# A decoder layer on one Trainium2 core: the first weight scales spread by one-hot matmuls, two weight products moved to GpSimd

## The chip, the core and the metric

The kernel runs on one core of a Trainium2 chip. A core has five engines that run on their own and wait for each other through semaphores: TensorE (PE; its weight loads are shown apart, as PEld), VectorE (DVE), ScalarE (ACT), GpSimd (POOL) and SyncE (SP), which here only issues transfers. ScalarE issues some transfers too. The on-chip memory SBUF has 128 partitions; TensorE writes its results to PSUM, which VectorE and ScalarE read. The metric is the time of one execution on the device in microseconds (us); lower is better. The time before is 569.73 us, the median of 3 runs (569.17 to 570.04).

## What is computed

A decoder layer on 1024 tokens (16 sequences of 64) of width 256, in f32: self-attention with 16 heads of 128, cross-attention to a context of width 64, and a mixture of 16 experts with 4 chosen per token, each behind a layer norm and added to its input. The change touches the first step alone, the projections of self-attention, whose weights come as codes with one scale for each block of 32 input rows:

```python
def _layernorm(x, axis=-1, eps=1e-05):
    m = jnp.mean(x, axis=axis, keepdims=True)
    v = jnp.var(x, axis=axis, keepdims=True)
    return (x - m) / jnp.sqrt(v + eps)

def _mxfp4_matmul(x, codes, scales, block_size=BLOCK):
    w = codes * jnp.repeat(scales, block_size, axis=0)
    return x @ w

q = _mxfp4_matmul(x, wq_codes, wq_scales) + bq
k = _mxfp4_matmul(x, wk_codes, wk_scales) + bk
v = _mxfp4_matmul(x, wv_codes, wv_scales) + bv
...
x = x + _L0_attn_ref(_layernorm(x, axis=-1), ...)
x = x + _L0_xattn_ref(_layernorm(x, axis=-1), ctx_512, ...)
x = x + _L0_ffn_ref(_layernorm(x, axis=-1), ...)
```

## The kernel before, in words

**Tiles.** The tokens lie in 8 tiles of 128 partitions by 256 features, taken in two halves of four tiles. The layer norm of a half (`layernorm_t`, L159) goes through: statistics of four tiles on VectorE (L170, L171), the variance plus epsilon (`ln_var`, L174), its power of -0.5 on GpSimd (`ln_rstd`, L177), `ln_shift` = -mean times `ln_rstd` on VectorE (L181), then the normed tiles `ln_x`, two on ScalarE and two on VectorE (L199, L192), eight 128x128 transposes on TensorE (L216), and for each 128 features a high part rounded on ScalarE (L222) and a low part, the rest, on VectorE (L224). TensorE multiplies both parts by the weights, so that little of f32 is lost.

**Weights of self-attention.** The heads go in groups of two. For each group the weights of q, k, v and o are `code` times `scale`, both 128 partitions by 512 columns (`multiply`, L509; the product at L514), on VectorE for q and k, and for v of the first group; otherwise on GpSimd. `load_weights` (L495) fetches both by SyncE: codes at L501, scales at L502. In memory the scales are held for 16 rows and spread over 128 partitions by the transfer, 8 partitions to a row. The pools hold three `code` and three `scale` tiles.

**Start.** Six transfers bring x, three from SyncE and three from ScalarE. TensorE has nothing to do yet and turns the identity over (`turn_idly`, L133): 22 transposes ahead of the real ones and 14 between the first half's transposes and its first product. `first_queries` (L612) is called inside the layer norm of the second half: it loads the first group's weights and begins the product of q with the first half (`head_qk_part`, L543, whose matmuls are at L104). After that the loop over heads runs: queries and keys (L551 is their bias on ScalarE), scores (L565), softmax (L324 to L334), transposes of the probabilities (L343), values (L582, L592), projection (L605).

**Order.** A planner places each instruction in its engine's queue when the program is built; `tc.issue_after`, used through `after` (L95), tells it to place an instruction behind another one. Each engine then works through its queue in this fixed order, so an instruction that waits holds up all behind it on its engine. A change in the first microseconds can also change the planner's choices later; it does so in the layer norm ahead of cross-attention, whose rope products are `rt` on VectorE (L976) and `roped` on GpSimd (L982), read by TensorE at L997.

**Names that the change touches.** `turn_idly(22)` at L137; `load_weights`, `multiply`, `first_queries`; `at_tile` (L89), the PSUM tiles of the scores, of which two exist; `raw_tile` (L359), raw weight tiles that are first used by cross-attention; the lists `variances`, `rstds`, `norms`, `scaled` and `lows`, in which `layernorm_t` records instructions for `after`.

## Time and profile before

| | |
|---|---|
| median of 3 runs | 569.73 us |
| the profiled execution | 570.74 us, of which 569.0 us are the span of its trace |
| granted TensorE clock, mean of the span | 0.984 |
| transfers by SyncE's queue | 58.71 MB, 34.7% of the 16 engines' span |
| transfers by ScalarE's queue | 1.05 MB, 0.6% |
| TensorE in the first 5 us / 5 to 10 / 10 to 15 / 15 to 20 | busy 1.86 / 5.00 / 4.03 / 5.00 us |
| TensorE's longest waits | 6.4 us in 2 for VectorE near the end, 3.1 us for the identity at the start |

The page of a profile gives busy times by engine, the span in 40 slices, the chain of waits that ended last, and groups of instructions. The trace behind it can be asked for a stretch of time. A row of the timeline reads: start and duration in us, engine, line, operation, output<-input, shape, count; then in brackets how long the engine stood idle before it and what it waited for. Instructions of one kind that follow each other are one row, with the time from the first one's start to the last one's end. A TensorE record is longer than the distance to the next one, since they overlap; distances tell the rate.

### The profile page before, as it was taken

How to read it: one execution, taken by the hardware profiler on the slowest of the kernel's cores; microseconds unless marked ns; L12 is line 12 of the kernel's file. 1: busy time of each engine (PE TensorE's matmuls, PEld its weight loads, DVE VectorE, ACT ScalarE, POOL GpSimd, SP SyncE). 2: the span in 40 equal slices, each digit the busy share in tenths (PEclk: the TensorE clock that was granted, in tenths of full speed). 3: DMA queues.
4: the chain of work that ended last, by engine and by line, in shares of the span. 5: the costliest groups of instructions: out<-in, count | busy, mean ns of one | idle time of the engine just before them, and what ended most of it. 6: DMA issues, size and time to landing. Idle time of an engine off the chain costs nothing.

```text
span 569.0 us, 10603 instructions
## 1 busy us (share of the span) xinstructions
PE 537.4 (94%) x4013; PEld 444.5 (78%) x4013; DVE 400.9 (70%) x879; ACT 279.3 (49%) x524; POOL 230.5 (41%) x213
## 2 busy tenths in 40 slices
PE   7999999999999998999999999999999879999961
PEld 6888898988989876667687676676788779999961
DVE  5456555644555788767485686888878678999876
ACT  4677556575565533131323324143445368777551
POOL 4160500102000104434441445453445738888862
PEclk9999999999999999999999999999999989999995
DMA  8654431724300499564010000000322667776374
GB/s 213 163 170 129 129 106 44 205 95 108 97 1 1 119 289 277 140 188 127 2 52 20 8 1 1 0 30 1 105 106 80 209 217 255 244 249 239 123 272 164
DMA packets 44262, 70.83 MB, mean 124 GB/s; under 512 B 11824, under 2 KB 25232, under 8 KB 44208
## 3 DMA queue, kind: packets, MB, share of 16 engines
q1 hardware_dynamic: 39376, 58.71, 34.7%
q0 software_dynamic: 3696, 10.36, 4.7%
q10 hardware_dynamic: 1136, 1.05, 0.6%
q8 instruction: 33, 0.54, 0.4%
q14 instruction: 21, 0.17, 0.1%
HBM read 48.61 MB, written 21.86 MB: 124 GB/s over the span
## 4 chain that ended last, share of the span: by engine, by line
PE 76%; DVE 11%; DMA 4%; issue 3%; ACT 3%; POOL 1%; SPq 0%; DVEq 0%; ACTq 0%; POOLq 0%
PE mm L104 45%; PE mm L997 7%; PE av L582 5%; PE at L565 4%; PE av L104 3%; PE at L343 3%; PE at L1020 2%; PE av L1033 2%; PE mm L431 2%; DMA yd<-y,to 2%; ACT w L278 1%; DMA w<-in_W 1%; DVE hp L113 1%; DVE w L283 1%; DVE x L1326 1%
## 5 line engine op out<-in xcount | busy, mean ns | idle before, releaser
L982 POOL TENSOR_TENSOR roped<-rt,rt 128x512 f32<-128x512 f32 x48 | 62.6, 1326 | 83.3 <-DVE rt L976 80.4
L976 DVE TENSOR_TENSOR rt<-mm,rope_q 128x512 f32<-128x512 f32 x96 | 61.4, 684 | 24.3 <-PE mm L104 23.6
L104 PE MATMUL mm<-xn,w_q 128*128 128x512 f32 x288 | 73.9, 403 | 0.5 <-ACT xn L222 0.5
L104 PEld LDWEIGHTS mm<-xn,w_q 128*128 128x128 f32 x288 | 52.2, 188 | 14.1 <-issue 1.8
L104 PE MATMUL mm<-xs,w 128*128 128x384 f32 x270 | 54.2, 348 | 6.0 <-ACT xs L112 3.0
L1296 POOL DMA_INDIRECT yd<-y,to x45 | 48.7, 1082 | 19.4 <-ACT y L1291 8.0
L104 PEld LDWEIGHTS mm<-xs,w 128*128 128x128 f32 x270 | 47.0, 193 | 8.3 <-ACT xs L112 4.0
L327 ACT ACTIVATE p<-p 128x512 f32<-128x512 f32 x32 | 20.1, 629 | 62.3 <-DVE p L326 62.3
L324 DVE TENSOR_REDUCE sm_m<-at 128x8 f32<-128x512 f32 x32 | 21.8, 680 | 36.1 <-PE at L565 35.2
L997 PE MATMUL mm<-roped,w_s 128*64 128x512 f32 x192 | 46.4, 601 | 0.7 <-POOL roped L982 0.7
L514 POOL TENSOR_TENSOR wv<-code,scale 128x512 fp32r<-128x512 f32 x7 | 9.0, 1282 | 87.4 <-DMA scale<-in_scales 50.3
L605 DVE TENSOR_TENSOR x<-mm,x 128x256 f32<-128x256 f32 x64 | 26.0, 419 | 24.0 <-PE mm L104 22.8
L104 PE MATMUL mm<-wo,o 128*128 128x256 f32 x256 | 39.6, 295 | 0.0
L104 PE MATMUL mm<-xn,wq 128*128 128x512 f32 x128 | 34.6, 404 | 0.7 <-ACT xn L222 0.5
L104 PE MATMUL av<-w,hp 128*128 128x256 f32 x225 | 35.0, 289 | 0.3 <-ACT y L1291 0.3
L104 PE MATMUL mm<-wv,xn 128*128 128x256 f32 x256 | 35.2, 288 | 0.0
L104 PE MATMUL mm<-xn,wk 128*128 128x512 f32 x128 | 34.9, 405 | 0.0
L582 PE MATMUL av<-pt,v 128*128 128x128 f32 x256 | 34.5, 277 | 0.0
L104 PEld LDWEIGHTS mm<-wo,o 128*128 128x128 f32 x256 | 32.9, 190 | 1.5 <-issue 0.4
L582 PEld LDWEIGHTS av<-pt,v 128*128 128x128 f32 x256 | 32.0, 191 | 1.2
L104 PEld LDWEIGHTS mm<-wv,xn 128*128 128x128 f32 x256 | 31.8, 189 | 0.9
L514 POOL TENSOR_TENSOR wo<-code,scale 128x512 fp32r<-128x512 f32 x8 | 10.9, 1368 | 52.0 <-PE mm L104 39.6
(216 smaller groups left out, 1163.8 us busy)
## 6 DMA issues: line engine op xcount, KB each, us to landing
w<-in_W SPq DMA_DIRECT2D x15, 640.0 KB, 4.2
code<-in_codes SPq DMA_DIRECT2D x32, 256.0 KB, 4.4
scale<-in_scales SPq DMA_DIRECT2D x32, 256.0 KB, 4.9
xr<-xd SPq DMA_DIRECT2D x15, 408.0 KB, 4.9
xd<-zeros SPq DMA_DIRECT2D x8, 720.0 KB, 6.8
yd<-zeros SPq DMA_DIRECT2D x8, 512.0 KB, 6.6
got<-yd SPq DMA_DIRECT2D x16, 256.0 KB, 3.6
wq<-in_Wq SPq DMA_DIRECT2D x4, 512.0 KB, 3.7
```

Source lines behind the costliest of these rows:

```text
L104: m = nc.tensor.matmul(ps, lhsT=l, rhs=r, start=(n == 0), stop=(n == len(pairs) - 1))
L324: nc.vector.tensor_reduce(m, sc, AX.X, ALU.max)
L327: exps.append(nc.scalar.activation(p, p, AF.Exp, scale=scale).ins)
L343: last = nc.tensor.transpose(ps[:, 2 * n : 2 * n + 2, :].rearrange("p a q -> p (a q)"), pn[:, 2 * n : 2 * n + 2, :].rearrange("p a k -> p ...
L514: mults[n] = eng.tensor_tensor(w, *loaded[gr].pop(n), ALU.mult).ins
L565: nc.tensor.matmul(sc[par * 64 : par * 64 + 64, 2 * g + pp, :], lhsT=qk[0][:, b * S : (b + 1) * S], rhs=qk[1][:, b * S : (b + 1) * S], sta ...
L582: nc.tensor.matmul(av[:, k * 128 : (k + 1) * 128], lhsT=v[:, i, k0 : k0 + HD], rhs=pt[:, i].rearrange("p a q -> p (a q)"), start=True, sto ...
L605: nc.vector.tensor_tensor(x[i], ps, x[i], ALU.add)
L976: nc.vector.tensor_tensor(mt, ps3, rope_table(t, 2 * ab + k), ALU.mult)
L982: nc.gpsimd.tensor_tensor(r.rearrange("p (b s) -> p b s", s=S), one, two, op)
L997: nc.tensor.matmul(ps[h // 2][(h % 2) * 64 : (h % 2) * 64 + 64], lhsT=w_s[:, t, blk, ab, :], rhs=roped[2 * t + ab], start=first[h], stop=l ...
L1296: sent = nc.gpsimd.indirect_dma_start(out=yd[: (E - 1) * SLOTS + min(TOPK, E - 1 - e) * NT], out_offset=bass.IndirectOffsetOnAxis(ap=to[:, ...
```

## The change

For the first group, `load_first_weights` takes the place of `load_weights`. The scales of q, k and v come as the four rows that they have for each 128 input rows, with a 4 by 128 block matrix that has a one in row r for the partitions 32r to 32r+31; two small transfers on ScalarE's queue fetch them into raw tiles. TensorE multiplies the block matrix by the four rows, which gives the scale of each partition, in PSUM, in two tiles used in turn. q's product reads its scales in PSUM. Those of k and v are copied to SBUF by ScalarE, and GpSimd multiplies these two weights. The first 22 idle transposes become 10 and another 8 that stand with the loads. The order of q's, k's and v's products is asked for behind other instructions than before.

```diff
-    turn_idly(22)
+    turn_idly(10)
...
+            def load_first_weights():
+                first = raw_tile("wkq", [4, 1, 640])
+                nc.scalar.dma_start(out=first[:, 0], in_=a["scales_first"][:, :640])
+                others = raw_tile("wq", [4, 2, 512])
+                nc.scalar.dma_start(
+                    out=others,
+                    in_=a["scales_first"][:, 640:].rearrange("r (n c) -> r n c", n=2),
+                )
+                for n, rows in (("q", first[:, 0, 128:]), ("k", others[:, 0]), ("v", others[:, 1])):
+                    code = sw.tile([128, 2, 256], F32, tag="code", name="code", bufs=3)
+                    loads.append(nc.sync.dma_start(out=code, in_=a["codes"][0, :, "qkvo".index(n)]).ins)
+                    scale = at_tile([128, 2, 256])
+                    nc.tensor.matmul(
+                        scale.rearrange("p c n -> p (c n)"),
+                        lhsT=first[:, 0, :128],
+                        rhs=rows,
+                        start=True,
+                        stop=True,
+                    )
+                    if n != "q":
+                        ps = scale
+                        scale = sw.tile([128, 2, 256], F32, tag="scale", name="scale", bufs=3)
+                        nc.scalar.copy(scale, ps)
+                    loaded.setdefault(0, {})[n] = code, scale
+                turn_idly(8)
+
             def multiply(gr, names, *order):
                 for n in names:
                     w = sw.tile([128, 2, 256], F32R, tag=f"w{n}", name=f"w{n}")
-                    eng = nc.vector if n in "qk" or n == "v" and gr == 0 else nc.gpsimd
+                    eng = nc.vector if n == "q" or n == "k" and gr else nc.gpsimd
...
             def first_queries(xn_h):
                 with after(turned[-1]):
                     turn_idly(14)
-                load_weights(0, "qk")
-                multiply(0, "q", variances[1])
-                multiply(0, "k", scaled[3], lows[1])
+                multiply(0, "q", norms[3])
+                multiply(0, "k", rstds[0])
                 nc.sync.dma_start(out=bqkv, in_=a["bqkv"])
-                load_weights(0, "v")
...
+            load_first_weights()
             xn_t = layernorm_t(1, meanwhile=first_queries)
-            multiply(0, "v", lows[3])
+            multiply(0, "v", rstds[1])
...
+    blocks = np.repeat(np.eye(4, dtype=np.float32), 32, axis=1)
+    arrays["scales_first"] = np.concatenate(
+        [blocks, arrays["scales"][0, :, :3].reshape(4, 3 * 512)], axis=1
+    )
     arrays["scales"] = np.repeat(arrays["scales"], 4, axis=1)
```

## The prediction

> **What bounds the kernel now.** I read the page's table of engines and the clock row first, then the chain of waits, then TensorE's waits by stage, then the timeline of the first 17 us (start, duration, engine, line, operation, count, and in brackets the idle time before it and who ended it).

> ```profile
> span 569.0 us, 10603 instructions
> PE 537.4 (94%) x4013; PEld 444.5 (78%) x4013; DVE 400.9 (70%) x879; ACT 279.3 (49%) x524; POOL 230.5 (41%) x213
> ```

> TensorE is the bound: busy for 537.4 of 569.0 us, and 76% of the chain. Its waits between 15 and 210 us add up to nothing; all its waiting lies before 14.04 us, around 211 to 228, and in the expert stage after 393. So whatever puts off the moment at which TensorE's unbroken stream begins puts off the end by as much, and only waits in those three places can be won. This is the beginning:

> ```profile
> 3.14 4.88 PE L135 MATMUL av<-ident 128*128 128x128 f32 x22 [3.14 <-POOL ident masks.py:199]
> 7.85 1.04 PE L216 MATMUL mm<-ident,ln_x 128*128 128x128 f32 x8
> 8.72 1.69 PE L135 MATMUL av<-ident 128*128 128x128 f32 x14
> 9.55 0.17 DVE L174 TENSOR_SCALAR ln_var<-ln_mv 128x4 f32<-128x4 f32 x1
> 9.74 0.69 DVE L514 TENSOR_TENSOR wq<-code,scale 128x512 fp32r<-128x512 f32 x1
> 9.79 1.50 POOL L177 TENSOR_TENSOR ln_rstd<-ln_var,half_power 128x4 f32<-128x4 f32 x1 [3.00 <-DVE ln_var L174]
> 10.35 1.28 DVE L224 TENSOR_TENSOR xn<-mm,xn 128x512 fp32r<-128x512 f32 x2
> 11.55 0.15 DVE L181 SCALAR_TENSOR_TENSOR ln_shift<-ln_mv,ln_rstd 128x4 f32<-128x4 f32 x1
> 11.79 1.09 ACT L199 ACTIVATE ln_x<-x,ln_shift,ln_rstd 128x256 f32<-128x256 f32 x2 [2.00 <-issue]
> 12.79 0.67 ACT L551 ACTIVATE qT<-mm,bqkv 128x512 f32<-128x512 f32 x1
> 13.40 1.08 ACT L222 CAST xn<-mm 128x512 fp32r<-128x512 f32 x2
> 14.04 0.50 PE L104 MATMUL mm<-xn,wq 128*128 128x512 f32 x1 [0.46 <-ACT xn L222]
> ```

> Read it backwards from 14.04: the stream begins when ScalarE has written the first high part of the second half (first of the two at 13.40). That waits on ScalarE for qT and the two ln_x, these for ln_shift on VectorE (11.55), this for the reciprocal deviation on GpSimd (9.79 to 11.29) and for VectorE's own queue. The weight transfers are not what ends last: VectorE was at ln_var until 9.72, and q's scales landed at 9.63 (2.63 plus 7.0 to landing); k's scales landed at 12.07, when VectorE was at ln_x until 12.47; v's at 14.55, and v's product stood at 15.23 behind other work. **The three scale loads are hidden, by 0.1, 0.3 and 0.7 us.**

> **The change, part by part.** The order of the built program gives what follows what on each engine.

> *Transfers.* Three loads of 256 KB leave SyncE's queue, two small ones (10 and 16 KB) join ScalarE's. That saves VectorE no wait (above). They cost ScalarE two issues of 0.4 us near 2.1 and 3.4, before its table load; it needs its first input at 7.03: nothing. Codes of k and v, bqkv and the next group land about 1 to 4 us earlier; nobody waits there: nothing. The small loads stand in the queue behind the last x load, issued at 1.66 and landed by 8.3 at the latest, where VectorE uses it; so I put them at 7.0 to 8.0.

> *VectorE.* It loses k's and v's products (0.68 each). The first lay before an idle 0.95, the second behind all that TensorE waits for: nothing. q's product now reads PSUM (0.68, as the 96 products at L976 that also read PSUM) and stands before ln_var instead of behind it, so ln_var ends at about 10.35 instead of 9.72. In exchange the reciprocal deviation, which took 1.50 beside that product and 1.04 without it, takes 1.04: it ends at 11.4 instead of 11.3. Nearly nothing.

> *Three one-hot products on TensorE,* f32, 4 rows by 512 columns, in its queue between the idle transposes and the real ones. The nearest row is the f32 product of 192 columns:

> ```profile
> L431 PE MATMUL mm<-wkq,wq x64: 323/326/431, 176.0 to 289.0; 128*128 128x192 f32 x64
> ```

> The 64 records stand for 32 products, each two records 0.16 apart, so 0.32 us for 192 columns and 0.86 for 512. [...]I take the row, since it is the same type; only its 128 rows differ. Of the idle transposes four go (18 instead of 22 ahead of the real ones, ending at 7.0 at the unwarmed spacing of 0.213). Then q's product, 7.5 to 8.5; four transposes (0.109 each); k's, 0.86; four more, to 10.2; 14 idle ones, 1.5; v's, to 12.6. [...]

> *Two more copies on ScalarE.* k's scales are copied ahead of the first half's high parts (10.0 to 10.6, moving these from 8.71 to 10.5), v's ahead of qT. By 11.5 the second high part is there, as the queues need; but the copy ahead of qT stands in the chain above: one 128x512 copy, +0.48 (the spacing of the two at L222).

> *GpSimd multiplies k's and v's weights,* 1.28 each (L514). k's stands right behind the second reciprocal deviation, and ln_shift on VectorE waits for that same instruction. ln_shift has two operands in SBUF. Where it ran beside a GpSimd product before, in the last layer norm:

> ```profile
> 372.91 0.93 DVE L181 SCALAR_TENSOR_TENSOR ln_shift<-ln_mv,ln_rstd 128x4 f32<-128x4 f32 x1
> ...
> 372.54 2.52 POOL L982 TENSOR_TENSOR roped<-rt,rt 128x512 f32<-128x512 f32 x2 [1.63 <-DVE rt L976]
> ```

> 0.93 instead of 0.15: it ended at 373.84, just when the first of the two GpSimd products (1.28 from 372.54) did. [...]GpSimd goes from one instruction to the next without a gap (that pair spans 2.52), so k's product is there first: it holds from 11.4 to 12.7, and ln_shift ends at 12.7 instead of 11.70. Behind it in VectorE's queue stand the second low part of half one and two ln_x, and ScalarE's ln_x wait too. Low parts, ln_x and L976 [...]keep their times (0.40 for ln_x at 374.96 beside the second roped product). **Sum at the start:** ln_x on ScalarE from 12.78 (11.79), two at 0.50, copy of v's scales 0.48, qT 0.62, high part 0.59: TensorE's stream begins at 15.53, **+1.5 us**. TensorE's own path (v's product to 12.6, four of q, transposes) would end at 15.1, so both causes nearly tie: without the lock it is +1.0 with these landings, without the products' length +1.5 still. If both are cheap, +0.2. v's product on GpSimd, after its copy at 14.3, ends at 15.6; TensorE asks for it at about 18.4.

> *What the scheduler moved elsewhere.* In the second layer norm eight rope products on VectorE now stand ahead of the half's ln_x, two of them where it idled:

> ```profile
> 219.66 0.16 DVE L181 SCALAR_TENSOR_TENSOR ln_shift<-ln_mv,ln_rstd 128x4 f32<-128x4 f32 x1 [1.12 <-POOL ln_rstd L177]
> 220.51 4.87 DVE L976 TENSOR_TENSOR rt<-mm,rope_q 128x512 f32<-128x512 f32 x8
> ...
> 225.14 1.94 PE L997 MATMUL mm<-roped,w_s 128*64 128x512 f32 x8 [0.16 <-POOL roped L982]
> 227.60 0.72 PE L997 MATMUL mm<-roped,w_s 128*64 128x512 f32 x2 [0.52 <-POOL roped L982]
> ```

> The four rope products that GpSimd's first pair needs are done at 221.2 instead of 222.9, so roped comes 1.3 us earlier and TensorE's two waits, 0.68 together, can go: **-0.68**. Late next are the half's transposes (ln_x at 224.3, asked for at about 226) and its low part (228.1, asked for at 228.9), both with room. Between 0.2 lost, if one of them is late, and 0.68 won; I take the win. The other moved instructions lie in the branch for overfull experts, of which this trace holds none: nothing.

> **Sum:** +1.49 - 0.68 = +0.8 us on the profiled execution's 569.0 of span (570.7 with what lies around it). The median shown is 569.7, so I carry the difference over: **570.5 us**.

> **Rivals.**
> - *The rope order doesn't pay* (a wait of like size takes its place): +1.5, 571.2. For it: the half's transposes now stand behind the first roped products. Against: they have over 1 us of room.
> - *The clock stays low longer.* The idle transposes run at 0.213 each until 7.7 and at 0.109 from there; fewer of them, then a product that waits for a transfer, could leave TensorE slow for some microseconds. q's and k's products then take 1.7 each, and eight transposes and 14 idle ones twice as long. Start +2.9, 572.0. Against: TensorE is asked for work nearly without a break.
> - *On the other side, not slower:* [...]k's scales on GpSimd come after ln_shift or the lock doesn't bite. Start +0.2, and with the rope gain -0.5: 569.3. Only the four-row operand speaks for it. It decides if the one-hot products are below about 0.4 and ln_shift ends by 11.8.
> - *The loads were the bound after all:* 256 KB less before q's product win it nothing, as VectorE is free at 9.5 at the earliest; at most 0.2 beyond the last case.

> **How the numbers follow.** A measurement tells about 0.2% (1.1 us) from no change. Chances: my sum 0.45, rope order without gain 0.23, slow clock 0.10, not slower 0.17, something else that gains more 0.05. My sum and the not-slower case fall mostly within 0.2%, the second and third mostly beyond: faster 0.08, same 0.50, slower 0.42. The range goes from the not-slower case to the slow clock: 569.2 to 572.2.

> **What would show it.** In the changed profile: ln_shift near 11.5 lasting about 1.2 us and ending with k's product on GpSimd (the lock); two records some 0.43 apart per one-hot product; TensorE's first unbroken high-part product at 15.5 (14.04 before); no wait for roped near 227. I am wrong at the start if that product begins before 14.8 or after 16.2, and wrong in the middle if waits between 211 and 232 don't shrink.

## The result, and the profile after

The changed kernel takes **575.08 us** (median of 20 runs, 570.74 to 579.28), the kernel before 569.71 (20 runs beside it, 568.74 to 571.47): ratio **1.0094, 95% interval 1.0073 to 1.0114**. It is slower, and its runs spread over 8.5 us where those of before spread over 2.7. The profiled execution took 576.15, its span is 574.4 (569.0 before). From the head of its page:

```profile
span 574.4 us, 10604 instructions
PE 542.5 (94%) x4015; PEld 445.3 (78%) x4015; DVE 399.5 (70%) x877; ACT 280.3 (49%) x526; POOL 234.1 (41%) x215
```

TensorE is busy 5.1 us longer with two records more, while its share stays 94%. So it did not wait more; something in it became slower. The timeline of the changed kernel's first 20 us (rows left out) shows where:

```profile
3.14 4.10 PE L135 MATMUL av<-ident 128*128 128x128 f32 x18 [3.14 <-POOL ident masks.py:199]
7.17 2.07 PE L523 MATMUL at<-wkq 4*128 4x512 f32 x2
9.17 1.12 PE L216 MATMUL mm<-ident,ln_x 128*128 128x128 f32 x4
10.22 2.07 PE L523 MATMUL at<-wq,wkq 4*128 4x512 f32 x2
12.22 1.11 PE L216 MATMUL mm<-ident,ln_x 128*128 128x128 f32 x4
12.33 0.59 ACT L533 COPY scale<-at 128x512 f32<-128x512 f32 x1 [4.18 <-PE at L523]
12.99 1.27 POOL L542 TENSOR_TENSOR wk<-code,scale 128x512 fp32r<-128x512 f32 x1 [1.69 <-ACT scale L533]
13.13 2.96 PE L135 MATMUL av<-ident 128*128 128x128 f32 x14
14.17 0.15 DVE L181 SCALAR_TENSOR_TENSOR ln_shift<-ln_mv,ln_rstd 128x4 f32<-128x4 f32 x1
16.02 1.12 PE L523 MATMUL at<-wq,wkq 4*128 4x512 f32 x2
17.07 1.20 PE L104 MATMUL mm<-xn,wq 128*128 128x512 f32 x4
18.10 1.04 PE L216 MATMUL mm<-ident,ln_x 128*128 128x128 f32 x8
18.30 0.69 ACT L579 ACTIVATE qT<-mm,bqkv 128x512 f32<-128x512 f32 x1 [0.54 <-PE mm L104]
19.70 0.50 PE L104 MATMUL mm<-xn,wq 128*128 128x512 f32 x1 [0.56 <-ACT xn L222]
```

The unbroken stream begins at 19.70 instead of 14.04: **+5.66 us**, with hardly a gap on TensorE from 3.14 on. Compare like rows: the one-hot product at 7.17 takes 2.07, that at 10.22 too, the third at 16.02 takes 1.12. The first group of four transposes takes 1.12, where before eight took 1.04; the 14 idle ones take 2.96 where they took 1.69. Everything up to 15.7 runs at about half the later speed. The trace's record of the granted clock says the same: its first entry is full speed from 15.71 us on, and from 7.81 in the kernel before.

One thing must be known to read these profiles: every view gives full clock for these first microseconds (9 in the page's clock row, 1.00 for a stretch), since the record has no entry before the first rise. Up to that rise the spacing of the transposes (0.213 us, later 0.109) tells the clock, not the view.

In the second layer norm, TensorE's waits between 200 and 240 us are now these, and the row for roped (0.7 us in two before) is gone:

```profile
PE mm L470 <- DVE x L633: 0.9, 1, 0.9
PE av L216 <- ACT ln_x L199: 0.6, 1, 0.6
PE mm L104 <- ACT xn L222: 0.5, 1, 0.5
```

Five landmarks, read off TensorE's rows, split the difference. Three later runs stand beside it: the changed kernel once more, a kernel before with 18 idle transposes in place of 22 that ran on the same chip as that, and the changed kernel with its products padded to 32 rows, on a third chip.

| TensorE begins (us) | before | changed | changed, second profile | 18 idle, its chip | padded to 32 rows, third run |
|---|---|---|---|---|---|
| the unbroken stream | 14.04 | 19.70 | 17.72 | 14.04 | 15.32 |
| the first product with roped | 225.14 | 230.18 | 228.21 | 225.11 | 225.81 |
| the last product with roped | 396.76 | 401.94 | 399.98 | 396.74 | 397.58 |
| the first transpose of gathered rows | 447.11 | 452.25 | 450.09 | 447.02 | 450.40 |
| end of the span | 568.97 | 574.38 | 570.45 | 567.01 | 570.33 |

Of the 5.66 lost at the start, 0.6 comes back in the second layer norm (5.04 late there), and the rest is carried to the end (5.41). The two kernels of one chip tell the same: 3.68 late at the start, 3.10 at the first product with roped, 3.44 at the end. Behind the last product with roped the chips differ: a kernel of a later experiment (nine 128-row products at the front), whose stream and last product with roped begin as before (14.03 and 396.77), begins the gathered rows at 449.66 on its chip. So the lower two rows of the last column can't be compared with the first.

### The profile page after: what moved, and what is told of

Its sections match the earlier page's. It is cut to its first block, busy times and chain, and to the rows that moved or that the text cites. A ratio compares the mean times of both kernels' runs of the same rounds, so it can differ in the third digit from the quotient of the medians.

```text
span 574.4 us, 10604 instructions
## 1 busy us (share of the span) xinstructions
PE 542.5 (94%) x4015; PEld 445.3 (78%) x4015; DVE 399.5 (70%) x877; ACT 280.3 (49%) x526; POOL 234.1 (41%) x215
## 3 DMA queue, kind: packets, MB, share of 16 engines
q0 software_dynamic: 3696, 10.36, 4.7%
q10 hardware_dynamic: 1152, 1.08, 0.6%
## 4 chain that ended last, share of the span: by engine, by line
PE 79%; DVE 8%; DMA 5%; issue 3%; POOL 3%; ACT 2%; SPq 0%; DVEq 0%; ACTq 0%; POOLq 0%
PE mm L104 44%; PE mm L1024 6%; PE av L610 5%; PE at L593 4%; PE av L104 4%; PE at L343 3%; PE at L1047 2%; PE av L1060 2%; PE mm L431 2%; POOL xd L861 2%; DMA xd<-rows,to 1%; PE av L135 1%; DMA w<-in_W 1%; DVE rt L1003 1%; PE mm L453 1%
## 5 line engine op out<-in xcount | busy, mean ns | idle before, releaser
L104 PE MATMUL mm<-xn,w_q 128*128 128x512 f32 x288 | 74.1, 403 | 0.5 <-ACT xn L222 0.5
L104 PEld LDWEIGHTS mm<-xn,w_q 128*128 128x128 f32 x288 | 52.2, 188 | 14.3 <-issue 2.7
L104 PE MATMUL mm<-xs,w 128*128 128x384 f32 x270 | 53.3, 343 | 7.1 <-ACT xs L112 3.7
L104 PEld LDWEIGHTS mm<-xs,w 128*128 128x128 f32 x270 | 45.8, 188 | 9.7 <-ACT xs L112 5.2
L542 POOL TENSOR_TENSOR wv<-code,scale 128x512 fp32r<-128x512 f32 x8 | 10.2, 1281 | 97.1 <-DMA scale<-in_scales 77.5
L104 PE MATMUL mm<-wo,o 128*128 128x256 f32 x256 | 39.6, 295 | 0.1
L104 PE MATMUL av<-w,hp 128*128 128x256 f32 x225 | 35.0, 290 | 0.6 <-ACT y L1318 0.6
L104 PE MATMUL mm<-wv,xn 128*128 128x256 f32 x256 | 35.2, 289 | 0.0
L104 PE MATMUL mm<-xn,wk 128*128 128x512 f32 x128 | 34.9, 405 | 0.0
L104 PE MATMUL mm<-xn,wq 128*128 128x512 f32 x128 | 34.3, 404 | 0.6 <-ACT xn L222 0.6
L104 PEld LDWEIGHTS mm<-wo,o 128*128 128x128 f32 x256 | 32.9, 190 | 1.5 <-issue 0.4
L104 PEld LDWEIGHTS mm<-wv,xn 128*128 128x128 f32 x256 | 31.8, 189 | 0.9
L104 PEld LDWEIGHTS av<-w,hp 128*128 128x128 f32 x225 | 30.4, 189 | 1.7 <-ACT y L1318 1.2
```

The lines of the kernel that those rows point to most:

```text
L104: m = nc.tensor.matmul(ps, lhsT=l, rhs=r, start=(n == 0), stop=(n == len(pairs) - 1))
```

## The experiments

### Rows of the one-hot products: 4, 128, 32

```diff
-                first = raw_tile("wkq", [4, 1, 640])
-                nc.scalar.dma_start(out=first[:, 0], in_=a["scales_first"][:, :640])
-                others = raw_tile("wq", [4, 2, 512])
+                first = raw_tile("wkq", [128, 1, 640])
+                nc.vector.memset(first, 0.0)
+                nc.scalar.dma_start(out=first[:4, 0], in_=a["scales_first"][:, :640])
+                others = raw_tile("wq", [128, 2, 512])
+                nc.vector.memset(others, 0.0)
...
-                    out=others,
+                    out=others[:4],
```

> The changed kernel with the operands of the three one-hot products padded with zeros to 128 rows (two clears on VectorE ahead of the two small loads); everything else as in the changed kernel, the products as long as before. Theory A [...]: the products now count, the clock is up by 9 us at the latest, TensorE's unbroken stream begins at about 15.5 us instead of 19.7, the time is 570 to 571 and the runs lie within 2 us of each other. Theory B (the products are long and stand in TensorE's queue; their rows don't matter to the clock): the clock is still low at 12 us, the stream begins near 19.7, the time is about 575 with the same wide spread.

Measured: 570.63 (14 runs), before 569.86 (43 runs); ratio 1.0014, interval 1.0001 to 1.0027. The same products, with 124 rows of zeros added, bring back most of the loss on this chip: 0.8 us over before instead of 5.4. (The runs lie within 4.2 us of each other, not within 2 as expected.) The clock rose at 6.40, and the timeline of this kernel has the first one-hot product at the high clock:

```profile
8.18 1.10 PE L525 MATMUL at<-wkq 128*128 128x512 f32 x2 [1.28 <-DMA wkq<-in_scales_first]
9.54 1.02 PE L525 MATMUL at<-wq,wkq 128*128 128x512 f32 x2
10.40 0.60 PE L216 MATMUL mm<-ident,ln_x 128*128 128x128 f32 x4
11.79 1.27 POOL L544 TENSOR_TENSOR wk<-code,scale 128x512 fp32r<-128x512 f32 x1
12.32 0.76 DVE L181 SCALAR_TENSOR_TENSOR ln_shift<-ln_mv,ln_rstd 128x4 f32<-128x4 f32 x1
15.84 0.50 PE L104 MATMUL mm<-xn,wq 128*128 128x512 f32 x1 [0.63 <-ACT xn L222]
```

The stream begins at 15.84. TensorE stood idle for 1.28 us ahead of the first product, inside the window from 6.40 to 9.81. It was busy for 2.13 of the 3.41 us, 62%, all of it with 128 rows, and the clock held: here a break of 1.28 us did not drop it.

Not all of the gain is the clock. From k's product to the transposes behind it are 0.86 us here (9.54 to 10.40), where the changed kernel's third product, at the high clock too, takes 1.05 (16.02 to 17.07). From the first one-hot product to v's it is 4.19 us here and 4.81 with 32 rows (third run), both with the clock up, so some 0.6 us of what padding to 128 rows wins is not the clock.

The twin on another chip, and the same with 32 rows, three times:

> The 128-row twin: ratio 1.0014 as on the first chip, between 1.000 and 1.003; clock up by 9.97 and no fall before the expert stage.

> The changed kernel with the operands of its one-hot products padded with zero rows to 32 instead of 128. If what counts is the number of rows with more than a few needed, 32 lies between: theory A1 ([...]32 of 128 rows is too little): clock up late as in the changed kernel, 573 to 577 us. A2 ([...]enough): as with 128 rows, 570.0 to 571.2 us.

> The changed kernel with operands padded to 32 rows, on another chip: the first chip had an expert stage that lasted 5 us longer in its profile, so that its 577.99 says little of the start. If 32 rows count: ratio 1.001 to 1.003, as with 128 rows. If not: 1.006 to 1.010, as in the changed kernel. Expected: the second, since its spread on the first chip (572.9 to 583.9) was as wide as the changed kernel's.

> Padded to 32 rows, beside the 128-row twin on one chip. Both profiles so far show the clock up at 7.0 and 7.8 and holding through the 32-row products, and cross attention's last product only 1.2 and 1.9 us later than before; their extra time lay in the first expert's stretch on a chip where that stretch is long for every kernel. If 32 rows hold the clock: ratio within 0.002 of the twin's. If the late rise does come in other runs: 0.004 to 0.008 above the twin's.

Measured: 128 rows again 1.0049 (1.0021 to 1.0076; 575.27 against 572.76), outside what was expected; 32 rows 1.0072 (1.0052 to 1.0092), 1.0072 (1.0031 to 1.0114) and, beside the 128-row twin, 1.0090 (1.0059 to 1.0121). By time 32 rows look like four. But all three profiles of 32 rows have an early clock (7.03, 7.77, 6.41) that holds; the last column of the table above is the third. Those profiled executions tell of the start only: the first two ran on a chip where the stretch from the first gathered rows to the third group of them (12.7 us before) took 20.2 and 15.7. The difference of the pair, 0.0041, lies at the lower edge of what a late rise in other runs would give, and the intervals overlap; 0.6 of its 2.3 us can be the longer products (above). **How many rows are needed stays open**, and so does why 128 rows cost 2.5 us on the second chip and 0.8 on the first: in its profile the clock was up at 6.84 and the stream began at 14.95, earlier than on the first.

### The same question without the change: nine products at the front

The kernel before, with its 22 idle transposes replaced by nine f32 products of the identity with itself; only the number of rows differs between these four kernels.

```diff
-    turn_idly(22)
+    for n in range(9):
+        nc.tensor.matmul(
+            idle[:, n % 4 * 128 : n % 4 * 128 + 128],
+            lhsT=ident[:4], rhs=ident[:4], start=True, stop=True,
+        )
```

> The kernel before, with its 22 idle transposes at the front replaced by nine f32 products of the identity's first four rows (128 output columns each, estimated 0.5 us each at the low clock, so that they end near 7.7 as the 22 did). No other part of the change is in it. Theory A [...]: the clock rises only some 3.4 to 7 us after the real transposes begin near 7.7, at 11.5 to 15.5 instead of 7.8; the stream starts 1.5 to 4 us later, 571.0 to 574.0 us in the median. Rival B (any product counts as work): clock up near 7.8, 569.4 to 570.3.

> The control to the four-row run: the same nine f32 products at the front, but of all 128 rows of the identity. Theory A: 128-row products count whatever the instruction is, clock up by about 7 to 9, 569.3 to 570.3 us. If it was the transpose mode that counted and f32 products don't, this run is as slow as its four-row twin (571 to 574).

The timeline of the four-row kernel:

```profile
3.14 4.21 PE L138 MATMUL av<-ident 4*128 4x128 f32 x18 [3.14 <-POOL ident masks.py:199]
7.74 1.97 PE L220 MATMUL mm<-ident,ln_x 128*128 128x128 f32 x8 [0.39 <-ACT ln_x L203]
9.50 2.69 PE L135 MATMUL av<-ident 128*128 128x128 f32 x14
```

and of its twin with 128 rows:

```profile
3.14 4.21 PE L138 MATMUL av<-ident 128*128 128x128 f32 x18 [3.14 <-POOL ident masks.py:199]
7.74 1.30 PE L220 MATMUL mm<-ident,ln_x 128*128 128x128 f32 x8 [0.39 <-ACT ln_x L203]
8.88 1.69 PE L135 MATMUL av<-ident 128*128 128x128 f32 x14
```

The first rows are the same to 10 ns in start and length: TensorE is busy from 3.14 to 7.35 in both. The clock rises at 8.21 behind 128 rows and at 11.55 behind four, one window later, and the eight transposes at 7.74 take 1.30 and 1.97. The windows lie nearly alike here (boundaries at 4.80 and 4.72), so this is the rows. Of the time A's expectation was missed: 572.83 and 572.88, with ratios of 1.0001 (0.9987 to 1.0016) and 0.9984 (0.9970 to 0.9998), not 1.5 to 4 us apart. The four-row kernel's stream starts at 14.46 against 14.03: here TensorE has room ahead of the stream, and a clock that is up by 11.5 costs 0.4. What cost in the changed kernel was a clock that stayed low through two products of 2.07 us each on TensorE's own path.

> The kernel before with nine f32 products of 16 identity rows at the front in place of its 22 idle transposes. Work of 128 rows follows from about 7.7 without much of a break. If 16 rows count as work, a window ends full by 9.97 at the latest and the clock rises there or earlier; if they don't, it can't rise before 10.4 [...] and rises by 14.5. Expected: they don't, 10.4 to 14.5.

> The same with 32 rows. If the share of rows sets it [...]: 32 of 128 is a quarter and too little, rise at 10.4 to 14.5. If [...]32 is enough: rise by 9.97, as with 128 rows (8.2).

> The same with 64 rows. If the share of rows sets it with a threshold near the 0.7 to 0.8 of a window seen with 128-row work, half the rows are too little: rise at 10.4 to 14.5. If [...]any larger product is enough: by 9.97.

First rise at 11.28, 11.43 and 11.51, as expected of products that don't count. (The 10.4 of the expectations is an estimate: a share between the 74% and the 80% below, of a window from 7.7 on; the 9.97 is 3.14 and two windows.) The windows up to 7.87, 8.02 and 8.10, each one window ahead of the rise, were filled to 85% by the 16-row products, to 80% by the 32-row ones, and to 82% by the 64-row ones with a first transpose, and no rise came behind them. Behind a window filled to 80% by work of 128 rows it came in another kernel (idle12, below), behind one of 74% it did not (idle18, below). So the 16-row products did not do what work of 128 rows did; for 32 and 64 the breaks of 0.6 to 1.0 us behind the products bring the test too near to these shares to decide. Their times (585.59, 577.25, 577.54, one run each, before 574.28 to 586.28 on that chip) tell nothing of the start.

### The number of idle transposes

> The kernel before, with 18 idle transposes ahead of the real ones instead of 22, and no one-hot products. If the four transposes that went are enough to keep the clock low (a break of 0.65 us before the real transposes), some runs begin late: median 0.5 to 2 us above the kernel before, with a spread of 2 to 3 us. If only the 4-row products keep it low, 569.7 and the narrow spread of the kernel before.

> The kernel before with 18 idle transposes, once more, as the twin of the rope-order kernel on the same chip: ratio 0.9985 as on the first chip, or 0.998 to 1.000.

The kernel before with `turn_idly(18)` for 22: 569.04 and 568.68, ratio 0.9985 both times (0.9977 to 0.9993 both times). The four transposes that the change takes away cost nothing; without them the kernel is even a little faster, and why is open. In the first of the two profiles the clock came up at 9.07, later than before, and the stream still began at 14.02; the window ahead of that rise was filled to 85%, the one before it to 74% (work from 3.14 to the boundary at 5.66).

> The changed kernel with 30 idle transposes ahead of the first one-hot product instead of 18. Theory A [...]: [...]the clock is up before the first product; each product takes 1.05 us; the products and transposes behind them start 1.5 to 2 us later than they could, so the stream begins at 16 to 17 us and the time is 571 to 572, with a spread below 2.5 us. Theory B (length of the products and of the queue ahead of them): 12 more transposes make it 1 to 2 us slower than the changed kernel, 576 to 577.

The changed kernel with 22 in the place of its first 10 idle transposes (30 in all ahead of the first product): 573.62, ratio 1.0068 (1.0047 to 1.0089), clock up at 6.95, stream at 16.84. The direction is A's, though on another chip and with an interval that overlaps the changed kernel's; the size is not A's (571 to 572, and a spread below 2.5 us where 3.8 were measured): the front transposes last to 8.47 in this profile even with the clock up on the way, instead of about 7.2, so a part of what the clock gives is spent on them. The clock held through its four-row products: the window from 6.95 to 10.36 had 1.93 us of 128-row work (57%) and 1.49 of four-row work.

> The changed kernel with 12 front idle transposes instead of 18: they last from 3.1 to 5.7 us, so no full window fits ahead of the first four-row product. Theory A: the clock never rises before 15 us; the fast end of the spread goes (the changed kernel's lowest run was 1.0018 times the median of before; here at least 1.006), median ratio 1.010 to 1.013, at or somewhat above the changed kernel's. Rival (it is the mere time of TensorE's three products that costs, the idle transposes mattering little): ratio as the changed kernel's, within 0.001, with the same lowest run.

With 4 in the place of 10 (12 in all): 577.58, ratio 1.0144 (1.0116 to 1.0172), lowest run 572.61, which is 1.0051 of before (at least 1.006 was expected). Fewer idle transposes make it worse, as A says, though its interval and that of the changed kernel on the same chip (next) just overlap. "Never before 15" was wrong: the clock rose at 13.92, behind a window whose first fifth still held a four-row product (transposes from 11.18 on, 80% of it). This rise did not take a full window.

### The changed kernel once more

> The changed kernel once more, unchanged, for a second profile and beside its twins on one chip. Theory A [...]: in this profile the rise is either at 6.4 to 7.1 us (a window fits into the front idle transposes, some 2 runs in 10) or at 15.4 or later, never between; ratio to before 1.007 to 1.012. Rival (the late rise was an accident of one profile): a rise anywhere between 7 and 15.

573.62, ratio 1.0093 (1.0062 to 1.0124). This profile is the clearest of all. TensorE's busy time in four windows, with the granted clock in the column PEclk:

```profile
core 0: us, PE busy (x), PEclk, DMA share, GB/s
3.31:6.72 3.41, 3.41 (x17) 1.00 0.94 296
6.72:10.13 3.41, 2.86 (x11) 1.00 0.78 223
10.14:13.55 3.41, 3.41 (x16) 0.50 0.45 160
13.55:16.96 3.41, 3.41 (x19) 1.00 0.69 228
```

and its timeline:

```profile
7.60 1.12 PE L523 MATMUL at<-wkq 4*128 4x512 f32 x2 [0.55 <-DMA wkq<-in_scales_first]
8.66 0.66 PE L216 MATMUL mm<-ident,ln_x 128*128 128x128 f32 x4
9.24 1.22 PE L523 MATMUL at<-wq,wkq 4*128 4x512 f32 x2
10.39 1.11 PE L216 MATMUL mm<-ident,ln_x 128*128 128x128 f32 x4
11.30 2.79 PE L135 MATMUL av<-ident 128*128 128x128 f32 x14
17.72 0.50 PE L104 MATMUL mm<-xn,wq 128*128 128x512 f32 x1 [0.57 <-ACT xn L222]
```

The first window lay whole within the idle transposes, and the clock rose at 6.72 (the row's 1.00 for that window itself is the missing record told of above; the clock was low in it). In the second TensorE was busy for 2.86 of 3.41 us, but only 0.9 of that with 128 rows; the clock **fell** at 10.14, the transposes at 10.39 take 1.11 instead of 0.66. In the third only a tail of a four-row product was left, and it rose again at 13.55. The expected "early or after 15.4, never between" missed the fall: in this profile the clock was not kept up either while four-row products were most of TensorE's work (1.96 of 2.86 us).

The break of 0.55 us in that window doesn't explain the fall, since the 128-row kernel held its clock through one of 1.28 (above), with TensorE busy for 62% of the window against 84% here. What the same order of work does with more rows is shown by the timeline of the second run with 32 rows, in its window from 7.77 to 11.19, behind which the clock stayed up:

```profile
7.90 1.09 PE L525 MATMUL at<-wkq 32*128 32x512 f32 x2 [0.66 <-DMA wkq<-in_scales_first]
8.93 0.66 PE L216 MATMUL mm<-ident,ln_x 128*128 128x128 f32 x4
9.52 1.12 PE L525 MATMUL at<-wq,wkq 32*128 32x512 f32 x2
10.57 0.66 PE L216 MATMUL mm<-ident,ln_x 128*128 128x128 f32 x4
```

(Its break lies almost wholly ahead of that window, and 1.2 us of its work there has 128 rows, against 0.9, so this pair alone would not be free of doubt.)

### The lock, and the rope order

> As the kernel with 128-row products, but k's and v's weights are multiplied on VectorE, ordered as in the kernel before. If the prediction's lock is real (ln_shift on VectorE waits for k's product on GpSimd), ln_shift ends about 1.0 us earlier than with these products on GpSimd, and the stream begins 0.4 to 0.5 us earlier, 0.4 us of the time. If the lock doesn't bite here, both kernels take the same time within 0.2 us.

The engine of the two products is changed and their order set back to that of the kernel before; of the edit, the engine's line:

```diff
-                    eng = nc.vector if n == "q" or n == "k" and gr else nc.gpsimd
+                    eng = nc.vector if n in "qk" or n == "v" and gr == 0 else nc.gpsimd
```

570.24, ratio 1.0008 (0.9997 to 1.0019), beside 1.0014 for the products on GpSimd. In this kernel's timeline ln_shift has nothing of GpSimd's beside it:

```profile
11.75 0.15 DVE L181 SCALAR_TENSOR_TENSOR ln_shift<-ln_mv,ln_rstd 128x4 f32<-128x4 f32 x1
13.06 0.69 DVE L544 TENSOR_TENSOR wk<-code,scale 128x512 fp32r<-128x512 f32 x1
```

0.15 instead of 0.76; above, it ended at 13.08, with the GpSimd product that ran from 11.79 to 13.06. What the prediction calls the lock is there: beside GpSimd's product ln_shift takes 0.61 us longer and ends 0.02 behind it. Which property of the two instructions makes it so was not shown. The medians differ by 0.4, which these intervals alone would not tell from nothing. Nor is the stream's earlier start in this profile (15.19 against 15.84) the lock's: v's one-hot product begins 0.57 earlier here (11.80 against 12.37), and from it to the stream are 3.39 us without the lock and 3.47 with it.

> The kernel before with 18 idle transposes, and with VectorE's order in the second layer norm's second half as the changed kernel has it (ln_shift behind two rope products, the ln_x behind eight). Theory (the rope order is worth TensorE's two waits for roped, 0.16 and 0.52 us): those waits are gone in the profile and the median is 0.5 to 0.8 us under that of the kernel with 18 idle transposes alone (569.0), so 568.3. Rival (a wait of like size takes its place): 568.8 to 569.3.

> The rope-order kernel beside its twin on the same chip. Its profile had the waits for roped gone, but the chip was another and lost more in the expert stage. Theory: 0.3 to 0.5 us at the end of cross attention is kept to the end, ratio 0.0005 to 0.0012 under its twin's. Rival (given back in the expert stage, whose waits on transfers take it up): the same ratio as its twin within 0.0004.

```diff
-            with after(*lows[:1] if which == 1 else ()):
+            with after(*lows[:1] if which == 1 else rts[1:2] if which == 2 else ()):
...
+                    with after(*rts[7:8] if which == 2 else ()):
+                        scaled.append(
```

The kernel with 18 idle transposes and the changed kernel's order around the rope products (`rts` lists these). The first run was on a chip with a long expert stage: 573.86, ratio 1.0007 (0.9990 to 1.0024). Beside its twin on one chip: 568.62 against 568.68, ratios 0.9988 and 0.9985. The waits for roped are gone in both profiles, and the landmarks show the gain: 0.61 at the first product with roped (224.50 against 225.11), 0.64 at the first gathered rows (446.38 against 447.02). At the end of the span 0.16 of it is left, and in the medians nothing can be told. That agrees with the rival, that the expert stage takes it back; one pair of profiles can't show more. What is faster than the kernel before, by 0.15%, is the kernel with 18 idle transposes, with or without this order.

## Why the prediction was wrong

The forecast was 570.5 with a range to 572.2; 575.08 was measured.

- *TensorE bounds, and the start of its stream sets the end*: right. 5.66 late at the start, 5.41 at the end; on another chip 3.68 and 3.44.
- *The scale loads were hidden*: nothing in the runs speaks against it; no kernel without their wait came out ahead of the one with 18 transposes.
- **The failed step is the clock.** The main sum laid TensorE's products from 7.5 to 12.6 at the high clock, as if the rise at 7.7 were given. It depended on what filled the window ahead of it (8.21 or 11.55 where the front products had 128 rows or four), and the change put four-row products there: the rise came at 15.71, and q's and k's products took 2.07 each where 0.86 was laid out. The rival "the clock stays low longer" named the effect, though as fewer transposes and a wait for a transfer, not as few rows. Its counter-argument, "TensorE is asked for work nearly without a break", was the wrong measure: in the second window of the second profile TensorE was busy for 84% and the clock fell. The rival had a chance of 0.10.
- *The rival's sum* was wrong too, and the range ended with it. Its own terms (two products 0.84 longer each, 22 transposes 0.104 longer each) make 4.0 us on TensorE's path, which the main sum lets end at 15.1: a start at 19.1, +5.0 instead of the +2.9 that it states, and 574.1 instead of 572.0.
- *The split of the 5.66*, by the third 32-row run, whose clock was up all along: its stream begins at 15.32, which is 1.28 over before; the changed kernel's first product came 0.34 later than its (7.17 and 6.83); the remaining 4.04 is the time that TensorE's rows between that product and v's one-hot product (16.02 and 11.64) took longer at half speed. So the forecast lacked these 4. The predicted +1.49 was near for a kernel whose clock is up (0.91 to 2.33 in the profiles of the padded kernels), in part by luck: it was reached along the lock's chain, and in the padded pair the lock adds only 0.1 to TensorE's own path.
- *The one-hot products*: 0.86 each, estimated from the f32 row, was near. At the high clock 0.86 is what 128 rows took to the next instruction; four rows took 1.05. Products below 0.4, which the rival on the other side asked for, were not seen.
- *The copy of scales on ScalarE*: there, 0.59 alone; hidden in the changed kernel, where qT waits for TensorE.
- *The lock*: ln_shift did take longer beside k's product on GpSimd and end with it (0.76 against 0.15 in the padded pair), though less than was foretold (1.2 long; 0.85 and 0.90 in two more padded profiles); in the changed kernel k's product came so late (12.99 to 14.26) that ln_shift at 14.17 met only its end and took 0.15. That low parts and `rt` keep their times beside GpSimd holds in the kernel before: two low parts took 1.28 at 225.30 and eight `rt` 4.87 at 220.51, with `roped` on GpSimd from 222.54 to 227.55.
- *The rope order*: both waits went as foretold and 0.6 is won there; that it lasts to the end of the kernel was not shown.

## What to carry to other kernels

A warm-up of TensorE is a thing that other instructions rest on: before putting small products near it, ask how many rows they read, since busy time alone did not keep the clock up here (it fell at 10.14, behind a window 84% busy). A product over few partitions can be padded with zero rows; with 128 it was even shorter here (0.86 us instead of 1.05), and on one chip that took most of the loss away, on another 2.5 us stayed. When a change makes the spread of the runs grow, look for something that depends on a phase, and take a second profile before believing in one.

## What was not expected of the hardware

- Products of four rows kept TensorE busy and did not raise its clock (rise at 11.55 against 8.21 for 128 rows, same start and length), nor did they keep it in one profile (a fall at 10.14, behind a window 84% busy); beside 1.93 us of 128-row work it held (30 idle transposes, 6.95 to 10.36).
- Windows that were not full were followed by a rise too: one with 80% of 128-row work and four-row work for the rest (12 idle transposes, rise at 13.92), and one with 85% and an idle rest (18 idle transposes, rise at 9.07). One with 74% was not (the window before that one).
- A clock that was up held through windows with less: 62% of 128-row work (128 rows, 6.40 to 9.81), and 57% with four-row products beside it (30 idle transposes). With 0.91 us of 3.41, 27%, and four-row products beside it, it fell. So it did with 54% in the expert stage of the kernel before (1.85 us of 128-row work from 461.77 to 465.18, then half clock until 468.60). No limit can be read off these few.
- A product of few rows took longer than one of 128: 1.05 us to the next instruction for 512 columns of f32 at the high clock, against 0.86.
- The spread of the changed kernel fits the phase: a window lies within the front transposes in some runs and not in others (rises at 15.71 and 6.72 in two profiles). That the single runs' times follow the phase was argued from this, not measured, as only profiled executions record the clock. Other causes of spread exist: the 128-row kernel on the second chip, clock up early in its profile, spread over 4.9 us.
- The clock also dropped for a window or more where TensorE waited in the expert stage: in the kernel before for one (above). On the chip with the longest stage, the 32-row kernel's timeline has

```profile
451.52 0.82 PE L1286 MATMUL at<-ident,xr 128*128 128x128 f32 x6
458.26 6.48 PE L104 MATMUL mm<-xs,w 128*128 128x384 f32 x18 [5.91 <-DVE x L969]
```

a wait of 5.91 us and then 18 records in 6.48 us; the clock was at half from 454.18 to 464.42. In the kernel before nine such records took 3.03 us at half clock (465.95) and 1.84 at full clock (456.69). So a late arrival cost more there than its own length; that this is why differences under 1 us made earlier did not always reach the end is the author's guess.
